# Layer 1 of a four-layer graph network: the new gate and the self terms worked out in the banks of their products

## The chip, the cores and the metric

The kernel runs on one core of a Trainium2 chip. The time is device time in microseconds (us), the median of several executions; lower is better. One execution was also taken by the hardware profiler. Engines: PE multiplies matrices (fp32 here), DVE and ACT work elementwise, POOL issues the indirect DMAs, SP issues plain ones. PE writes to PSUM, which has eight banks of 128 x 512 fp32 numbers; POOL and the DMAs work on SBUF and DRAM.

## The reference

Four layers over one graph of 6250 nodes and 106250 edges, each with a layer norm and a relu ahead of it and a residual. The change lies in layer 1 and in the products for layer 2 that the same loop makes:

```python
# layer 1, h = relu(layernorm(x)); both directions of every edge are in the list
input_in  = segment_mean((h @ W_in.T + b_in)[src], dst)
input_out = segment_mean((h @ W_out.T + b_out)[dst], src)
gi = concat(input_in, input_out) @ W_ih.T + b_ih
gh = h @ W_hh.T + b_hh
reset = sigmoid(i_r + h_r);  inp = sigmoid(i_i + h_i)
new = tanh(i_n + reset * h_n)
x = x + (1 - inp) * h + inp * new

# layer 2, h = relu(layernorm(x)); 8 relations r
hW = einsum('nd,rde->rne', h, weight)
x = x + h @ sl_w.T + sl_b + segment_sum(hW[edge_type, src], dst) / max(deg, 1)
```

All tensors are fp32 with 256 features.

## The kernel before, in words

The nodes are sorted by their number of edges into 49 blocks of 128, and each block has a fixed number of slots per node (CAPS, 39 down to 9, 822 in all; a node's edge to itself is left out of the slots). After a stage that builds the lists, stages f0 to f3 are the layers 0 to 3. In each stage POOL issues one indirect DMA for each block and slot (L1110): 128 rows of a table in DRAM, one to each partition.

Stage f1 is layer 1. The two weight matrices of each direction have been folded into one, wc. The blocks are taken from the one with fewest slots to the one with most. Five steps, written as generators, stand a block apart, so that in round k block k is summed, block k-1 multiplied, and so on:

- sums: eight gathers fill a buffer v (seven buffers); DVE adds the rows in a tree (L1383, L1386, L1390), and compares neighbour lists for a check of the graph ("mirror": L1176, and L1181 to L1188 at the block's end).
- products: the total is scaled (L1399, L1400) and a bias row made (L1402); PE transposes h and the total; then PE makes the gate products pg (h and total, 512 columns), ph and pi (256 columns each: h's and the total's part of the new gate), each in a PSUM tile of kind "g".
- gates: DVE adds biases (L1425, L1427, L1428), ACT takes the sigmoid, DVE works out the new gate (L1434, L1435, after ACT's tanh L1438, L1439), adds it to the residual xt (L1433, L1440), and takes the statistics of the next norm; ACT makes h2 (L1452).
- messages: PE transposes h2 and multiplies it by the weights of the eight relations, two at a time (L1462), and ACT moves each pair out of PSUM into res (L1463), which SP stores to DRAM for layer 2's gathers. Then PE makes the own product (L1468), and DVE adds its bias and the product to xt (L1470, L1471).
- selves: a node's edges to itself: for each of eight relations DVE adds res times a factor per node to xt (L1476). SP stores xt (L1480).

The order on PE, DVE and ACT is the order in which the program is written (manual_schedule), with waits put in by the framework; L1492 lists, by letters s, p, g, m and o, how the steps of a round are dealt out, and L1494 what finishes them. POOL and SP run ahead as buffers allow. The eight PSUM banks of f1 are two of kind "t" (transposes), three of kind "g" and three of kind "m" (messages and the own product). At the end of f1 "judge" (L1216) sums up the check; layer 2's first gather comes after it.

Of the kernel before, what the change touches and what calls it, by code (L numbers as in the profile page):

```python
# [8 lines left out]
F32 = mybir.dt.float32  # L9
# [3 lines left out]
ALU = mybir.AluOpType  # L13
# [4 lines left out]
P = 128  # L18
# [8 lines left out]
D = 256  # L27
H = 8
DH = 32
R = 8  # L30
# [1189 lines left out]
def sparse(ctx: ExitStack, tc: tile.TileContext, S, qv_d, rows_d, wc_d, bc_d, b_ih, w_hh,  # L1220
           b_hh, w_rel, w_sl, b_sl, w_gat, att_src, att_dst, b_gat, gamma, beta, out):

    nc = tc.nc
    K = Fast(ctx, tc)
# [125 lines left out]


    rel_idx = K.c([P, NB, J], I32, "rel_idx")
    with K.stage("f1", t=2, g=3, m=3), tc.tile_pool(name="f1w", bufs=1) as wp, tc.tile_pool(name="f1", bufs=2) as pool:
        wc = K.weights(wp, wc_d, "wc")
        wh = K.weights(wp, w_hh, "w_hh")
        wr = K.weights(wp, w_rel, "w_rel")
        ws = K.weights(wp, w_sl, "w_sl")
        bc = K.row(wp, bc_d.rearrange("a n -> (a n)"), 3 * D, "bc")
        bi = K.row(wp, b_ih, 3 * D, "b_ih")
        bh = K.row(wp, b_hh, 3 * D, "b_hh")  # L1360
        nc.vector.tensor_add(bi[:, : 2 * D], bi[:, : 2 * D], bh[:, : 2 * D])
        bs = K.row(wp, b_sl, D, "b_sl")
        rel_rows = rel_d[: NP * R, :].rearrange("(n r) d -> n (r d)", r=R)
        mirror = Mirror(K, S, wp)
        state = {}

        nothing = lambda *a: iter(())
        order = list(range(NB - 1, -1, -1))

        def sums(i):  # L1370

            h = pool.tile([P, D], F32, name="hb", tag="hb", bufs=4)
            nc.sync.dma_start(h, K.block(h1_d, i)[:, :D])
            xt = pool.tile([P, D], F32, name="xb", tag="xb", bufs=7)
            nc.sync.dma_start(xt, K.block(x1_d, i))
            total = pool.tile([P, D], F32, name="total", tag="total", bufs=3)
            state[i] = dict(h=h, xt=xt, ins=total)
            for c, n in S.chunks(i, 8):
                v = S.fill(pool, "v", 7, h1_d, i, c, n, 8, HW, S.idx)
                m = n  # L1380
                while m > 2:
                    k = m // 2
                    nc.vector.tensor_add(v[:, :k, :D], v[:, :k, :D], v[:, m - k: m, :D])  # L1383
                    m -= k
                if m == 2:
                    nc.vector.tensor_add(total if c == 0 else v[:, 0, :D], v[:, 0, :D], v[:, 1, :D])  # L1386
                elif c == 0:
                    nc.vector.tensor_copy(total, v[:, 0, :D])
                if c:
                    nc.vector.tensor_add(total, total, v[:, 0, :D])  # L1390
                mirror.found(i, c, n, v[:, :n, D:])
                yield
            mirror.block(i)

        def products(i):

            h, ins = state[i]["h"], state[i]["ins"]

            nc.vector.scalar_tensor_tensor(ins, h, S.own[:, i: i + 1], ins, op0=ALU.mult, op1=ALU.add)  # L1399
            nc.vector.tensor_scalar(ins, ins, S.rcnt[:, i: i + 1], None, op0=ALU.mult)  # L1400
            ba = pool.tile([P, 3 * D], F32, name="ba", tag="ba")
            nc.vector.scalar_tensor_tensor(ba, bc, S.has[:, i: i + 1], bi, op0=ALU.mult, op1=ALU.add)  # L1402
            yield
            pt = K.ps([P, 4, P], "t")
            for k in range(4):
                nc.tensor.transpose(pt[:, k, :], (h, ins)[k // 2][:, k % 2 * P: (k % 2 + 1) * P], K.ident)
            both = pool.tile([P, 4, P], F32, name="hit", tag="hit")
            nc.scalar.activation(both, pt, AF.Copy)
            ht, it = both[:, :2, :], both[:, 2:, :]
            yield  # L1410
            pg = K.ps([P, 2 * D], "g")
            K.product(pg, ht, wh[:, :, : 2 * D], stop=False)
            K.product(pg, it, wc[:, :, : 2 * D], start=False)
            ph = K.ps([P, D], "g")
            K.product(ph, ht, wh[:, :, 2 * D:])
            pi = K.ps([P, D], "g")
            K.product(pi, it, wc[:, :, 2 * D:])
            state[i].update(ba=ba, pg=pg, ph=ph, pi=pi)

        def gates(i):  # L1420

            x = state[i]
            h, xt, ba = x["h"], x["xt"], x["ba"]
            g = pool.tile([P, 2 * D], F32, name="g", tag="g")
            nc.vector.tensor_add(g, x["pg"], ba[:, : 2 * D])  # L1425
            new = pool.tile([P, D], F32, name="new", tag="new")
            nc.vector.tensor_add(new, x["ph"], bh[:, 2 * D:])  # L1427
            nc.vector.tensor_add(ba[:, 2 * D:], ba[:, 2 * D:], x["pi"])  # L1428
            yield
            nc.scalar.activation(g, g, AF.Sigmoid)  # L1430
            yield

            nc.vector.tensor_add(xt, xt, h)  # L1433
            nc.vector.tensor_mul(new, new, g[:, :D])  # L1434
            nc.vector.tensor_add(new, new, ba[:, 2 * D:])  # L1435
            nc.scalar.activation(new, new, AF.Tanh)
            yield
            nc.vector.tensor_sub(new, new, h)  # L1438
            nc.vector.tensor_mul(new, new, g[:, D:])  # L1439
            nc.vector.tensor_add(xt, xt, new)  # L1440
            st = pool.tile([P, 6], F32, name="st", tag="st")
            nc.vector.bn_stats(st, xt)
            mv = pool.tile([P, 2], F32, name="mv", tag="mv")
            nc.vector.bn_aggr(mv, st)
            rs = pool.tile([P, 1], F32, name="rs", tag="rs")
            nc.scalar.activation(rs, mv[:, 1:2], AF.Sqrt, bias=K.eps)
            yield
            nc.vector.reciprocal(rs, rs)
            nm = pool.tile([P, 1], F32, name="nm", tag="nm")
            nc.vector.tensor_scalar(nm, mv[:, 0:1], rs, -1.0, op0=ALU.mult, op1=ALU.mult)  # L1450
            h2 = pool.tile([P, D], F32, name="h2", tag="h2")
            nc.scalar.activation(h2, xt, AF.Relu, bias=nm, scale=rs)  # L1452
            x["h2"] = h2

        def messages(i):
            x = state[i]
            x["h2t"] = K.transposed(pool, x["h2"], "h2t")
            yield
            res = x["res"] = pool.tile([P, R, D], F32, name="res", tag="res")
            for r in range(0, R, 2):  # L1460
                pm = K.ps([P, 2 * D], "m")
                K.product(pm, x["h2t"], wr[:, :, r * D: (r + 2) * D])  # L1462
                nc.scalar.activation(res[:, r: r + 2, :].rearrange("p a b -> p (a b)"), pm, AF.Copy)  # L1463
                if r == 2:
                    yield
            nc.sync.dma_start(K.block(rel_rows, i), res.rearrange("p r d -> p (r d)"))
            pm = K.ps([P, D], "m")
            K.product(pm, x["h2t"], ws)  # L1468
            yield
            nc.vector.tensor_add(x["xt"], x["xt"], bs)  # L1470
            nc.vector.tensor_add(x["xt"], x["xt"], pm)  # L1471

        def selves(i):
            xt, res = state[i]["xt"], state[i]["res"]
            for r in range(R):
                nc.vector.scalar_tensor_tensor(xt, res[:, r, :], S.ownr[:, i, r: r + 1], xt, op0=ALU.mult,  # L1476
                                               op1=ALU.add)
                if r == 3:
                    yield
            nc.sync.dma_start(K.block(x2_d, i), xt)  # L1480
            del state[i]

        with tc.manual_schedule(engines={nc.tensor.engine, nc.vector.engine, nc.scalar.engine}):
            for k in range(NB + 4):
                s, p, g, m, o = (f(order[k - d]) if 0 <= k - d < NB else nothing()
                                 for d, f in enumerate((sums, products, gates, messages, selves)))
                if k == 4:  # L1490
                    nc.vector.scalar_tensor_tensor(rel_idx, S.idx, float(R), S.types, op0=ALU.mult, op1=ALU.add)
                for step in (g, p, m, p, g, s, m, g, o, s, m, p, g, s, o, g):  # L1492
                    next(step, None)
                for step in (s, m, p, g, o):  # L1494
                    for _ in step:
                        pass
            mirror.judge(S.bad, S.todo)
# [3 lines left out]
    with K.stage("f2", t=2, m=4, a=2), tc.tile_pool(name="f2w", bufs=1) as wp, tc.tile_pool(name="f2", bufs=2) as pool:  # L1501
        w = K.weights(wp, w_gat, "w_gat")
# [4 lines left out]
        for i in range(NB):  # L1507
# [6 lines left out]
            xt = pool.tile([P, D], F32, name="xb", tag="xb")  # L1514
# [7 lines left out]
            pm = K.ps([P, D], "m")  # L1522
# [11 lines left out]
    with K.stage("f3", m=2, a=2, w=2), tc.tile_pool(name="f3w", bufs=1) as wp, tc.tile_pool(name="f3", bufs=2) as pool:  # L1534
# [3 lines left out]
        o = wp.tile([P, NB, D], F32, name="o", tag="o")  # L1538
# [6 lines left out]
        for i in range(NB):  # L1545
            n = P if i < NB - 1 else NLAST
# [246 lines left out]
```

## Time and profile before

| what | value |
|---|---|
| median of 3 runs | 5667.33 us (5661.75 to 5673.34) |
| the profiled execution's own time | 4971.87 us |
| its span, first to last instruction | 4970.0 us |
| busy share of the span | POOL 69%, PE 61%, DVE 55%, ACT 17% |
| gathers of layer 1, first start to last end | 1578.9 to 2686.6 us |
| first gather of layer 2 | 2744.9 us |

The profiled execution is 14% shorter than the runs that were timed; the profile has no record of those, so its durations are of the profiled one alone. A line of a group reads: line, engine, operation, what it writes <- what it reads (partitions x elements), count | busy us, mean ns of one | idle time ahead of it and who ended it. A line of the timeline reads: start us, length us, engine, line, operation.

### The profile page before, as it was taken

What the parts mean: (1) busy time and instruction counts of PE and PEld (TensorE: products, weight loads), DVE (VectorE), ACT (ScalarE), POOL (GpSimd) and SP (SyncE); (2) the same over time, 40 slices, a digit from 0 to 9 for tenths busy, and PEclk for the clock granted to TensorE, in tenths of its full rate; (3) what the DMA queues carried; (4) which work ended last, traced back from release to release, by engine and by line L of the source; (5) the groups of instructions that cost most, each with busy time, mean ns of one, the idle gap of its engine ahead of it and who ended that gap; (6) DMA issues with size and microseconds to landing.
All of it is one profiled execution on the core that took longest, in us unless ns stands there. A gap on an engine that the chain in (4) does not pass through costs nothing. (4 is left out here: it accounts for less than half of the span.)

```text
span 4970.0 us, 34096 instructions
## 1 busy us (share of the span) xinstructions
PE 3019.2 (61%) x9191; PEld 1861.4 (37%) x9192; DVE 2730.3 (55%) x5064; ACT 865.4 (17%) x1808; POOL 3444.3 (69%) x3538
## 2 busy tenths in 40 slices
PE   5863544444444888776555778788873555555560
PEld 4532433333333444433322334344441444444450
DVE  6853888888886889877766111111121434343443
ACT  1231111222222444333222000000110000000000
POOL 1254777777774777777774677777776777777766
PEclk9976777777766898887777676766776777777785
DMA  3446777888885566555553344444445444444431
GB/s 106 120 157 202 224 231 233 233 237 236 239 238 167 182 191 190 181 170 170 169 159 112 119 121 119 122 123 125 127 128 164 110 112 115 114 115 115 116 101 52
DMA packets 328336, 776.03 MB, mean 156 GB/s; under 512 B 87439, under 2 KB 172299, under 8 KB 321607
## 3 DMA queue, kind: packets, MB, share of 16 engines
q0 software_dynamic: 196864, 595.62, 42.3%
q1 hardware_dynamic: 110904, 162.80, 9.4%
q10 hardware_dynamic: 20367, 15.35, 1.0%
q8 instruction: 76, 1.25, 0.1%
q14 instruction: 125, 1.02, 0.1%
HBM read 638.29 MB, written 135.19 MB: 156 GB/s over the span
## 5 line engine op out<-in xcount | busy, mean ns | idle before, releaser
L1110 POOL DMA_INDIRECT v<-h,rec_in x822 | 856.7, 1042 | 250.7 <-issue 232.1
L1110 POOL DMA_INDIRECT v<-rel,rel_idx x822 | 782.8, 952 | 308.5 <-issue 238.9
L1110 POOL DMA_INDIRECT v<-xa,rec_in x822 | 779.1, 948 | 268.7 <-issue 227.9
L1110 POOL DMA_INDIRECT qv<-qv,rec_in x822 | 779.2, 948 | 255.4 <-issue 200.8
L1513 PE MATMUL ps_a<-v,ident 128*128 128x256 f32 x1644 | 767.7, 574 | 206.4 <-DMA v<-rel,rel_idx 189.9
L1513 PEld LDWEIGHTS ps_a<-v,ident 128*128 128x128 f32 x1644 | 351.2, 258 | 587.5 <-DMA v<-rel,rel_idx 532.8
L1571 PE MATMUL ps_a<-v,ident 128*128 128x256 f32 x1644 | 449.5, 435 | 33.3 <-DVE v L1569 33.3
L1297 PE MATMUL ps_a<-qv,ident 128*128 128x256 f32 x1644 | 454.0, 444 | 8.7 <-DVE qv L1295 8.6
L1292 PE MATMUL ps_a<-row,ident 128*128 128x256 f32 x98 | 59.7, 713 | 628.1 <-DVE row L1291 628.1
L538 PE MATMUL ps_m<-w_rel,h2t 128*128 128x512 f32 x784 | 426.5, 706 | 1.1 <-ACT h2t L531 1.1
L1297 PEld LDWEIGHTS ps_a<-qv,ident 128*128 128x128 f32 x1644 | 370.0, 229 | 108.3 <-DVE qv L1295 43.9
L1571 PEld LDWEIGHTS ps_a<-v,ident 128*128 128x128 f32 x1644 | 362.9, 223 | 118.6 <-DVE v L1569 56.4
L1553 DVE TENSOR_TENSOR s<-v,asd 128x64 f32<-128x64 f32 (+7 forms) x124 | 26.4, 213 | 604.1 <-DMA v<-xa,rec_in 595.9
L1259 DVE TENSOR_TENSOR tmp<-qv,ps_k 128x1280 f32<-128x1280 f32 (+4 forms) x183 | 247.0, 1350 | 178.1 <-ACT ps_k L1253 85.1
L1383 DVE TENSOR_TENSOR v<-v 128x512 f32<-128x512 f32 (+2 forms) x211 | 187.6, 889 | 184.1 <-DMA v<-h,rec_in 157.6
L1292 PEld LDWEIGHTS ps_a<-row,ident 128*128 128x128 f32 x98 | 24.5, 310 | 647.9 <-DVE row L1291 574.0
L1527 DVE TENSOR_TENSOR tmp<-att,xa 128x512 f32<-128x512 f32 x49 | 34.2, 697 | 416.7 <-ACT xa L1525 416.7
L538 PEld LDWEIGHTS ps_m<-w_rel,h2t 128*128 128x128 f32 x784 | 178.9, 235 | 217.5 <-issue 205.7
L1566 PE MATMUL ps_a<-xh,ident 128*128 128x256 f32 x98 | 49.2, 598 | 342.5 <-DVE xh L1564 260.5
L1260 DVE TENSOR_REDUCE s<-tmp 128x40 f32<-128x1280 f32 (+4 forms) x183 | 247.1, 1351 | 6.3
L1516 DVE SCALAR_TENSOR_TENSOR xb<-ps_a,rcnt_in,xb 128x256 f32<-128x256 f32 x49 | 23.7, 483 | 409.8 <-PE ps_a L1513 409.8
L1295 DVE TENSOR_TENSOR qv<-qv,ps_w 128x1280 f32<-128x1280 f32 (+4 forms) x183 | 235.0, 1344 | 0.0
(285 smaller groups left out, 4555.8 us busy)
## 6 DMA issues: line engine op xcount, KB each, us to landing
rel<-res SPq DMA_DIRECT2D x49, 1024.0 KB
rows<-mrow SPq DMA_DIRECT2D x49, 512.0 KB
fx<-xb SPq DMA_DIRECT2D x147, 128.0 KB
qv<-qv,rec_in POOLq DMA_INDIRECT x822, 3.8
v<-h,rec_in POOLq DMA_INDIRECT x822, 3.1
v<-rel,rel_idx POOLq DMA_INDIRECT x822, 2.7
v<-xa,rec_in POOLq DMA_INDIRECT x822, 2.8
qv<-mrow ACTq DMA_DIRECT2D x49, 256.0 KB
```

The lines of the kernel that those rows point to most:

```text
L538: self.nc.tensor.matmul(out, xt[:, k, :], w[:, k, :], start=start and k == 0, stop=stop and k == n - 1)
L1110: self.nc.gpsimd.indirect_dma_start(out=out, out_offset=None, in_=table, in_offset=bass.IndirectOffsetOnAxis(ap=idx, axis=0))
L1259: nc.vector.tensor_mul(tmp[:, :n, :], qv[:, :n, :D], pk[:, None, :].to_broadcast([P, n, D]))
L1260: nc.vector.tensor_reduce(s[:, c: c + n, :], tmp[:, :n, :].rearrange("p j (h d) -> p j h d", h=H), axis=AX.X, op=ALU.add)
L1292: nc.tensor.matmul(pm, K.ident, row[:, 2, :], start=True, stop=False)
L1295: nc.vector.tensor_mul(v, v, w[:, c: c + n, :, None].to_broadcast([P, n, H, DH]))
L1297: nc.tensor.matmul(pm, K.ident, qv[:, j, D: 2 * D], start=False, stop=c + j == nd - 1)
L1383: nc.vector.tensor_add(v[:, :k, :D], v[:, :k, :D], v[:, m - k: m, :D])
L1513: nc.tensor.matmul(pa, K.ident, v[:, j, :], start=c + j == 0, stop=c + j == nd - 1)
L1527: nc.vector.tensor_mul(tmp, att, xa[:, None, :D].to_broadcast([P, 2, D]))
L1566: nc.tensor.matmul(pm, K.ident, xh, start=True, stop=False)
L1571: nc.tensor.matmul(pm, K.ident, v[:, j, :D], start=False, stop=c + j == nd - 1)
```

## The change

```diff
-    with K.stage("f1", t=2, g=3, m=3), ...
+    with K.stage("f1", t=2, g=3, m=2, w=1), ...
...
-            ph = K.ps([P, D], "g")
+            both = K.ps([P, 2 * D], "g")
+            ph, pi = both[:, :D], both[:, D:]
             K.product(ph, ht, wh[:, :, 2 * D:])
-            pi = K.ps([P, D], "g")
             K.product(pi, it, wc[:, :, 2 * D:])
...
-            new = pool.tile([P, D], F32, name="new", tag="new")
-            nc.vector.tensor_add(new, x["ph"], bh[:, 2 * D:])
+            new = x["ph"]
+            nc.vector.tensor_add(new, new, bh[:, 2 * D:])
...
             nc.sync.dma_start(K.block(rel_rows, i), res.rearrange("p r d -> p (r d)"))
-            pm = K.ps([P, D], "m")
+            yield
+            pm = x["pm"] = K.ps([P, D], "w")
             K.product(pm, x["h2t"], ws)
             yield
-            nc.vector.tensor_add(x["xt"], x["xt"], bs)
-            nc.vector.tensor_add(x["xt"], x["xt"], pm)
+            nc.vector.tensor_add(pm, pm, bs)
+            nc.vector.tensor_add(pm, pm, x["xt"])

         def selves(i):
-            xt, res = state[i]["xt"], state[i]["res"]
+            xt, pm, res = (state[i][n] for n in ("xt", "pm", "res"))
             for r in range(R):
-                nc.vector.scalar_tensor_tensor(xt, res[:, r, :], S.ownr[:, i, r: r + 1], xt, op0=ALU.mult,
-                                               op1=ALU.add)
+                nc.vector.scalar_tensor_tensor(pm if r < R - 1 else xt, res[:, r, :], S.ownr[:, i, r: r + 1], pm,
+                                               op0=ALU.mult, op1=ALU.add)
...
-                for step in (g, p, m, p, g, s, m, g, o, s, m, p, g, s, o, g):
+                for step in (g, p, m, p, g, s, m, g, o, s, m, p, g, o, s, m, g):
                     next(step, None)
-                for step in (s, m, p, g, o):
+                for step in (s, o, m, p, g):
```

The new gate has no SBUF tile of its own any more: it is worked out, tanh included, in the half bank where its product with h lies, and the two 256-column products share a bank. The own product has a bank of its own ("w"), in which bias, xt and seven of the self terms are added; the eighth writes the sum to xt in SBUF. The messages' banks are two. In a round, the second half of the self terms comes ahead of the third step of the sums, and the own product, a step of its own now, after that and so behind the products of the next block.

More of the change, by code (lines that the diff above doesn't have):

```diff
@@ L1352, in sparse @@
     rel_idx = K.c([P, NB, J], I32, "rel_idx")
-    with K.stage("f1", t=2, g=3, m=3), tc.tile_pool(name="f1w", bufs=1) as wp, tc.tile_pool(name="f1", bufs=2) as pool:
+    with K.stage("f1", t=2, g=3, m=2, w=1), tc.tile_pool(name="f1w", bufs=1) as wp, tc.tile_pool(name="f1", bufs=2) as pool:
         wc = K.weights(wp, wc_d, "wc")
```

## The prediction, made before the changed kernel was run

> **What bounds the kernel now.** The chain that ended last is no help here (it names only the last scatter), so I read the page's busy shares, then its costliest groups, then the stretches of layer 1, the waits in it, and its timeline.
>
> ```profile
> PE 3019.2 (61%) x9191; PEld 1861.4 (37%) x9192; DVE 2730.3 (55%) x5064; ACT 865.4 (17%) x1808; POOL 3444.3 (69%) x3538
> ...
> L1110 POOL DMA_INDIRECT v<-h,rec_in x822 | 856.7, 1042 | 250.7 <-issue 232.1
> L1110 POOL DMA_INDIRECT v<-rel,rel_idx x822 | 782.8, 952 | 308.5 <-issue 238.9
> L1110 POOL DMA_INDIRECT v<-xa,rec_in x822 | 779.1, 948 | 268.7 <-issue 227.9
> L1110 POOL DMA_INDIRECT qv<-qv,rec_in x822 | 779.2, 948 | 255.4 <-issue 200.8
> ```
>
> Each of the four layers issues the same 822 gathers on POOL. In layer 1 (v<-h) one takes 1042 ns on average, elsewhere about 950.
>
> ```profile
> core 0: us, PE busy (x) PEld busy (x) DVE busy (x) ACT busy (x) POOL busy (x), PEclk, DMA share, GB/s
> 1578.90:2060.00 481.10, 375.51 (x1006) 193.44 (x1006) 409.86 (x911) 186.70 (x309) 371.61 (x378) 0.87 0.63 196
> 2060.00:2686.60 626.60, 382.42 (x970) 197.01 (x970) 458.80 (x964) 181.53 (x300) 485.80 (x463) 0.76 0.55 165
> 2686.60:2744.90 58.30, 33.78 (x84) 16.36 (x84) 39.62 (x89) 17.32 (x27) 0.00 (x1) 0.79 0.17 66
> ```
>
> The stretches are layer 1's short blocks, its long blocks, and the drain between its last gather and layer 2's first. DVE is busiest (85%) in the first, yet POOL never waits for it:
>
> ```profile
> POOL v L1110 <- issue: 232.1, 761, 0.5
> ...
> DVE v L1383 <- DMA v<-h,rec_in: 157.6, 44, 6.1
> ...
> POOL v L1110 <- DVE todo L1216: 58.3, 1, 58.3
> ...
> DVE same L1186 <- ACT own_slots L1183: 26.2, 22, 1.5
> ```
>
> POOL's gaps are issue gaps of 0.3 us; its one real wait is the 58.3 us drain. Layer 1 lasts 822 gathers x (0.945 + 0.305) = 1027 us, plus what stretches gathers, plus the drain. The first gather starts at 1578.9 and the last ends at 2686.6: 1107.7 us, so the stretching is 80 us. What stretches them is in the timeline:
>
> ```profile
> 2143.35 0.42 DVE L1439 TENSOR_TENSOR new<-new,g 128x256 f32<-128x256 f32 x1
> ...
> 2143.41 1.18 POOL L1110 DMA_INDIRECT v<-h,rec_in  x1 [0.30 <-issue]
> ...
> 2150.09 0.94 POOL L1110 DMA_INDIRECT v<-h,rec_in  x1 [0.30 <-issue]
> 2150.15 0.68 DVE L1425 TENSOR_TENSOR g<-ps_g,ba 128x512 f32<-128x512 f32 x1
> ...
> 2152.33 1.00 DVE L1402 SCALAR_TENSOR_TENSOR ba<-bc,has_in,b_ih 128x768 f32<-128x768 f32 x1
> ...
> 2152.60 1.55 POOL L1110 DMA_INDIRECT v<-h,rec_in  x1 [0.30 <-issue]
> ```
>
> A gather that reaches a point about 0.126 us after its start while DVE is inside an operation with two SBUF inputs stops until that operation ends. L1439 ends at 2143.77: 2143.77 - 2143.41 - 0.126 = 0.23, and the gather is 1.18 - 0.945 = 0.23 too long. L1402: 2153.33 - 2152.60 - 0.126 = 0.60; measured 0.60. L1425 has one input in PSUM; its gather is not stretched. Over the whole timeline, 304 of the 822 gathers run more than 20 ns over 945, and this rule gives each one's excess within 30 ns. Operations with a PSUM input (L1425, L1427, L1428, L1471) cover that point 63 times and stretch none.
>
> **What the skill says.** The Trainium skill, "SBUF — State Buffer", section "Who interferes with whom": "A DVE instruction with two SBUF inputs contends with a GpSimd instruction that reads SBUF"; the first to come holds the shared ports for its whole length, and one with at most one SBUF input, outside the two-port modes, does not contend. The trace agrees, number for number (above). "VectorE: DVE Perf Modes", "Rules for kernel authors", has elementwise work on a PSUM operand at one element a cycle; the trace agrees that this costs fp32 nothing:
>
> ```profile
> L1476 DVE SCALAR_TENSOR_TENSOR xb<-res,ownr,xb 128x256 f32<-128x256 f32 x392 | 191.2, 488 | 10.9
> ...
> L1516 DVE SCALAR_TENSOR_TENSOR xb<-ps_a,rcnt_in,xb 128x256 f32<-128x256 f32 x49 | 23.7, 483 | 409.8 <-PE ps_a L1513 409.8
> ```
>
> L1516 is the after-form of a self term, bar the output. In layer 2 it covers the gathers' point 18 times and stretches none.
>
> **The change, part by part.**
>
> *Inputs to PSUM.* Each block turns 14 DVE operations from two SBUF inputs into one of SBUF and one of PSUM: L1434, L1435, L1438, L1439, L1440, L1470 and the eight of L1476. Their count stays. Giving every stretched gather to the operation that covers its point, they hold: L1476 12.0 us (75 gathers), L1439 6.8 (29), L1435 2.3 (20), L1440 0.5, L1438 0.3, L1470 0.3; together 22.2 us. Others keep 58: L1383 31.6, L1402 14.5, L1176 3.1, the rest under 2.2 each. POOL bounds the stage, so a stretch removed is time removed: **-22.2**. A second estimate: if phases were even, an operation of length L would catch L²/(2 x 1.25) of stretch. Over the rows that is 58 us for the changed ones (392 x 0.095 + 294 x 0.071) and 125 for those that stay (81 L1383 of 1.22 us: 48; 100 of 0.69: 19; 49 L1402: 20; 259 adds of 0.42: 18; small ones 20). Measured is 80 of 183, a share of 0.44; 125 x 0.44 = 55 stays, so -25. I take the direct count, since a gather that arrives earlier may just wait longer for the same end of L1402 or L1383.
>
> *In-place in PSUM.* Reading and writing one bank in one DVE instruction is not in the trace. Writing alone is: L1288 into PSUM took 299 ns at 128 elements, L1277 into SBUF 293. Lower bound -10 ns each; upper +267 ns (a second pass over 256 elements), for 14 writes 3.7 us a block. I take +6 ns: 0.1 us a block, hidden, as DVE has room. A chunk's buffer is free 37 us or more before POOL writes it again (the least: 1738.6 to 1775.6, the end of the seventh earlier L1176 against the first gather). At the upper bound the 22 short blocks would cost 82 us, less 26 us of waits (next part), less 37 of room: 19 us reach POOL, and the gain is nearly gone. Tanh from PSUM to PSUM: ACT's 256-element copies took 384 ns out of PSUM and 369 into it, against 408: no cost.
>
> *The moved steps.* The second half of the self terms goes ahead of the third step of the sums. In the 22 short blocks that step is the mirror's, which waits on ACT (26.2 us over 22 times); 2.04 us of self terms now fill this. DVE shortens, POOL doesn't care: 0. On SP, L1480's store is issued a little earlier, in the same order against L1466 and the loads: 0.
>
> *The own product* moves behind the next block's products on PE, and waits for the last self term to free its one bank. Queued behind it are the transposes of h2, which wait for L1450 and L1452 anyway, later on DVE and ACT than that self term. L1470 now waits for it: PE ends the own product about where the gate products ended before, 0.3 to 2.7 us ahead of L1470 in short blocks, over 3.6 in long ones. Cost 0, or at most some 0.8 us of DVE in seven blocks, inside the 37 us. In the drain nothing covers it: L1470 (0.42), done early before, now follows the last product, and in the round with the last gate products L1425 comes later, pushing L1434 by about 0.3. **+0.8**, between 0 and 3.
>
> *Banks.* Two for the messages: the third pair needs the first one's eviction. In the tightest case seen that ends at 1720.0 and the third pair begins at 1720.2; PE has 207.7 us of waits on h2. 0. New and input products share one bank, so three "g" banks hold one and a half blocks; the bank wanted was freed a round earlier. 0.
>
> Sum: -22.2 + 0.8 = **-21.4**. The profiled execution took 4971.87 us (span 4970.0), so its successor should take 4950. The runs' median, 5667.33, is 695 us above it and the profile doesn't show why; I carry the difference over unscaled (scaled by 5667/4972 it would be -24): 5667.3 - 21.4 = 5646.
>
> **Rivals.** About 0.2% (11 us) is what a measurement of this kernel can tell from no change.
> - *The rest takes it back* (no change, 5663): gathers come earlier at L1402 and L1383 and are let go at the same ends. At a share of 0.6, 75 us remain: -5 + 0.8. For it: L1402 covers 41 points in 49 blocks. Against: layer 2's two such operations (13 us if even) show 5.3, a share of 0.40.
> - *More than counted* (5629): reordered DVE work leaves a share of 0.33, 41 us: -39 + 0.8. For it: short blocks follow a period set by DVE (18.6 to 19.5 us), which the filled ACT wait shortens.
> - *Slower* (5688): the same re-phasing the other way. Now the 0.69 us adds catch 0.6 us of an even 19, because they follow the 1.22 us ones at once; if gathers fall evenly on L1383 and L1402, a share of 0.8 leaves 100 us: +20 + 0.8. It decides from 0.73 on (91 us); break-even is 0.63.
>
> **How the numbers follow.** Forecast 0.58 (own range 5634 to 5656), taken back 0.18, more 0.12, slower 0.12. Faster 0.58 + 0.12 = 0.70; same 0.18; slower 0.12. The range 5625 to 5670 takes in the first three cases (and the in-place bound) and leaves out the slower one and some tails.
>
> **What would show it.** Right: the v<-h gathers' mean falls from 1042 to about 1015 ns, no L1434 to L1440, L1470 or L1476 stretches one, their own lengths stay within 10 ns, and the drain is 58 to 61 us. Wrong: that mean unchanged with L1402 and L1383 stretching more; in-place operations of 0.6 us and more, with POOL waiting for L1176; or PE's own product ended late before L1470.

## The result, and the profile after

The changed kernel took 5734.58 us (median of 4 runs, 5725.62 to 5744.7), the kernel before 5670.34 us (4 runs, 5661.75 to 5677.82) in the same rounds: a ratio of 1.011, with a 95% interval of 1.0086 to 1.0134. It is 64 us slower; the forecast was 21 us faster, with a range that ended at 5670.

One thing has to be known to read any number below: the same program takes one of two quite different times, and all the runs of a set, which share a chip, take the same one. In the six sets of runs below the kernel before had medians of 4972.2, 5605.6, 4972.3, 4972.3, 5659.1 and 4970.0 us, on the chips numbered 13, 6, 12, 1, 9 and 1. I call the first kind of chip short and the second long. That the chip itself decides it is likely but not shown: only chip 1 was met twice, short both times. By its time, the profile of before that the prediction was made from is of the short kind; the timed runs of the result, and the profile after (5739.23 us, span 5737.4), are of the long kind.

The page of the changed kernel, the same lines as were shown of before: busy shares, then the four layers' gathers (out <- in, count | busy us, mean ns of one | idle us ahead of them, and what ended most of it).

```profile
PE 2816.1 (49%) x9191; PEld 1880.0 (33%) x9192; DVE 2737.6 (48%) x5064; ACT 862.9 (15%) x1808; POOL 3396.5 (59%) x3538
...
L1110 POOL DMA_INDIRECT v<-h,rec_in x822 | 802.3, 976 | 559.0 <-DVE hits L1176 289.1
L1110 POOL DMA_INDIRECT v<-rel,rel_idx x822 | 785.8, 956 | 485.3 <-issue 232.6
L1110 POOL DMA_INDIRECT v<-xa,rec_in x822 | 780.4, 949 | 423.5 <-issue 229.9
L1110 POOL DMA_INDIRECT qv<-qv,rec_in x822 | 780.7, 950 | 417.6 <-issue 369.8
```

Two things are to be seen. In layer 1 (v<-h) a gather takes 976 ns instead of 1042, so most of the stretching that the change was priced on is gone. But POOL's idle time there is 559 us instead of 251, and in layers whose code did not change it is 155 to 177 us more as well (417.6 against 255.4 for qv). No engine is busy for more than 59% of the span. The waits of layer 1 (in total, times, longest, us):

```profile
PE ps_t L1406 <- DVE total L1400: 383.7, 37, 30.6
ACT h2t L531 <- remote: 338.0, 32, 29.6
POOL v L1110 <- DVE hits L1176: 289.1, 38, 15.0
DVE ps_w L1472 <- remote: 243.3, 29, 17.1
...
POOL v L1110 <- DVE todo L1216: 77.0, 1, 77.0
```

The third line is new against the profile before: POOL stops for the buffers v, which DVE gives back with L1176. The fourth names the longest of DVE's own waits: it stands at L1472, the first addition to the own product. "Remote" means that the releasing signal came at a moment at which the profile has no instruction ending. One such place in the timeline:

```profile
1943.42 1.03 PE L538 MATMUL ps_w<-w_sl,h2t 128*128 128x256 f32 x4
...
1944.28 0.38 PE L529 MATMUL ps_t<-ident,h 128*128 128x128 f32 x2
...
1944.50 0.38 PE L1406 MATMUL ps_t<-ident,hb 128*128 128x128 f32 x2
...
1948.06 0.95 POOL L1110 DMA_INDIRECT v<-h,rec_in  x1 [0.30 <-issue]
1950.81 0.43 DVE L1472 TENSOR_TENSOR ps_w<-ps_w,b_sl 128x256 f32<-128x256 f32 x1 [7.70 <-issue]
...
1951.59 0.38 ACT L531 ACTIVATE h2t<-ps_t 128x256 f32<-128x256 f32 x1 [7.85 <-remote]
...
1953.52 0.35 DVE L1400 TENSOR_SCALAR total<-total,rcnt_in 128x256 f32<-128x256 f32 x1
...
1953.93 0.69 PE L1406 MATMUL ps_t<-ident,total 128*128 128x128 f32 x2 [9.05 <-DVE total L1400]
```

The own product is recorded as ended at 1944.45 and the transposes of h2 at 1944.66, yet DVE starts on the one at 1950.81, 6.4 us later, and ACT on the other at 1951.59, 6.9 us later (for the first the profile names no releaser, for the second a remote one). The ends of matrix products in a profile are modelled, so by themselves these lines cannot tell a product that was finished late from one whose signal came late; the count further down comes back to this. Meanwhile PE has nothing to do: its next instruction waits for the total (L1400), which stands behind L1472 in DVE's queue. DVE waits for PE's last result and PE for DVE, until the signal comes.

The nearest counterpart is the kernel before on a long chip (the run b_fourth below, one execution of 5645.36 us, on chip 9). Its gathers and its waits in layer 1:

```profile
L1110 POOL DMA_INDIRECT v<-h,rec_in x822 | 844.9, 1028 | 442.5 <-issue 239.0
...
L1110 POOL DMA_INDIRECT qv<-qv,rec_in x822 | 780.5, 950 | 411.1 <-issue 372.3
```

```profile
PE ps_t L1406 <- DVE total L1400: 239.9, 28, 32.1
...
ACT h2t L531 <- remote: 213.0, 15, 32.3
POOL v L1110 <- DVE hits L1176: 196.1, 25, 18.2
...
POOL v L1110 <- DVE todo L1216: 93.8, 1, 93.8
...
DVE g L1425 <- remote: 82.9, 10, 14.8
...
DVE ba L1428 <- remote: 52.8, 12, 10.1
...
DVE new L1427 <- remote: 34.0, 8, 6.3
```

So before stops POOL there too. From layer 1's first gather to its last it took 1290.1 us, the changed kernel 1364.1 in its profile. The 74.0 us between them: the gathers' own time 802.3 - 844.9 = -42.6; pauses of POOL over 0.4 us 325.9 - 203.8 = +122.1; and 18 fewer plain gaps of 0.305, -5.5. The change did what it set out to do to the gathers, and nearly three times as much came back as stops. These are single executions of two runs, not made side by side; the ratio above is the measurement, the split only shows its kind.

### The profile page after: what moved, and what is told of

The parts are those of the page before. It is cut to its first block, busy times and chain, and to the rows that moved or that the text cites. A ratio compares the mean times of both kernels' runs of the same rounds, so it can differ in the third digit from the quotient of the medians.

```text
span 5737.4 us, 34048 instructions
## 1 busy us (share of the span) xinstructions
PE 2816.1 (49%) x9191; PEld 1880.0 (33%) x9192; DVE 2737.6 (48%) x5064; ACT 862.9 (15%) x1808; POOL 3396.5 (59%) x3538
## 5 line engine op out<-in xcount | busy, mean ns | idle before, releaser
L1110 POOL DMA_INDIRECT v<-h,rec_in x822 | 802.3, 976 | 559.0 <-DVE hits L1176 289.1
L1110 POOL DMA_INDIRECT qv<-qv,rec_in x822 | 780.7, 950 | 417.6 <-issue 369.8
L1297 PE MATMUL ps_a<-qv,ident 128*128 128x256 f32 x1644 | 510.1, 467 | 224.3 <-issue 200.8
L1573 PE MATMUL ps_a<-v,ident 128*128 128x256 f32 x1644 | 472.8, 441 | 132.4 <-issue 114.1
L538 PE MATMUL ps_m<-w_rel,h2t 128*128 128x512 f32 x784 | 454.7, 742 | 109.2 <-ACT res L1464 68.6
L1297 PEld LDWEIGHTS ps_a<-qv,ident 128*128 128x128 f32 x1644 | 388.8, 240 | 354.9 <-issue 261.6
L1515 PE MATMUL ps_a<-v,ident 128*128 128x256 f32 x1644 | 455.0, 431 | 64.7 <-issue 50.3
L538 PEld LDWEIGHTS ps_m<-w_rel,h2t 128*128 128x128 f32 x784 | 185.0, 246 | 346.6 <-issue 258.7
L1406 PE MATMUL ps_t<-ident,total 128*128 128x128 f32 x98 | 31.8, 424 | 440.9 <-DVE total L1400 383.7
L1571 DVE TENSOR_TENSOR v<-v,ps_w 128x2048 f32<-128x2048 f32 (+7 forms) x124 | 232.9, 1914 | 0.0
L538 PE MATMUL ps_m<-w_gat,ht 128*128 128x256 f32 x196 | 81.7, 560 | 305.1 <-ACT ht L531 175.2
L529 PE MATMUL ps_t<-ident,h 128*128 128x128 f32 x196 | 48.1, 333 | 344.4 <-ACT h L521 235.0
```

What stands on the lines that cost most here:

```text
L529: nc.tensor.transpose(pt[:, k, :], x[:, k * P: (k + 1) * P], self.ident)
L538: self.nc.tensor.matmul(out, xt[:, k, :], w[:, k, :], start=start and k == 0, stop=stop and k == n - 1)
L1110: self.nc.gpsimd.indirect_dma_start(out=out, out_offset=None, in_=table, in_offset=bass.IndirectOffsetOnAxis(ap=idx, axis=0))
L1297: nc.tensor.matmul(pm, K.ident, qv[:, j, D: 2 * D], start=False, stop=c + j == nd - 1)
L1515: nc.tensor.matmul(pa, K.ident, v[:, j, :], start=c + j == 0, stop=c + j == nd - 1)
L1571: nc.vector.tensor_mul(vv, vv, w[:, c: c + m, :, None].to_broadcast([P, m, H, DH]))
```

## The experiments

The theory, called the order theory below: on a long chip signals of PE come late, and the late own product makes DVE and PE wait for each other. Its rivals: two message banks are too few (bank theory); the sums held in the banks cost something (in-place, gate or self theory); or the change is slower on any chip. The expectations call the two kinds of chip conditions, and the rule of the stretched gathers the ports theory. Which kind of chip a set would meet could not be chosen, so some kernels appear in several sets. Every set has its own runs of the kernel before.

**First set, a short chip: before as it is, and the parts alone.** Before is unchanged in b_again. The run called gate has the new gate in its bank, which its two products share, and nothing else:

```diff
-            ph = K.ps([P, D], "g")
+            both = K.ps([P, 2 * D], "g")
+            ph, pi = both[:, :D], both[:, D:]
             K.product(ph, ht, wh[:, :, 2 * D:])
-            pi = K.ps([P, D], "g")
...
-            new = pool.tile([P, D], F32, name="new", tag="new")
-            nc.vector.tensor_add(new, x["ph"], bh[:, 2 * D:])
+            new = x["ph"]
+            nc.vector.tensor_add(new, new, bh[:, 2 * D:])
```

The run called order has only the banks and the order:

```diff
-    with K.stage("f1", t=2, g=3, m=3), ...
+    with K.stage("f1", t=2, g=3, m=2, w=1), ...
...
-            pm = K.ps([P, D], "m")
+            yield
+            pm = x["pm"] = K.ps([P, D], "w")
...
-                for step in (g, p, m, p, g, s, m, g, o, s, m, p, g, s, o, g):
+                for step in (g, p, m, p, g, s, m, g, o, s, m, p, g, o, s, m, g):
...
-                for step in (s, m, p, g, o):
+                for step in (s, o, m, p, g):
```

The run called self is order with the self terms summed in the own product's bank (new lines alone):

```diff
+            nc.vector.tensor_add(pm, pm, bs)
+            nc.vector.tensor_add(pm, pm, x["xt"])
...
+                nc.vector.scalar_tensor_tensor(pm if r < R - 1 else xt, res[:, r, :], S.ownr[:, i, r: r + 1], pm,
```

Expected of b_again:

> The kernel before, unchanged, profiled again beside the others. Theory P (the profile that the prediction was read from shows an execution that differs from the timed ones): its span comes out near 5670 us and not near 4970, its matmuls start tens of us after their gathers as in the changed kernel's profile, and layer 1's gathers take about 1290 us from first to last (1364 in the changed kernel, less the 64 us by which that is slower). Rival (the changed kernel alone has these waits): a span near 4970 and gathers of layer 1 in about 1108 us.

Of gate:

> Only the new gate is worked out in PSUM (new and input products in one bank); self terms, message banks and order as before. Ports theory (a gather waits for a vector operation with two SBUF inputs, and that is what counts): 5 to 10 us faster than before, about 5662. Order theory (the loss comes from the own product behind the next block's products, on which the vector engine then waits): no change, 5670 within 11 us. If the in-place work in PSUM itself were slow: slower by 10 us or more.

Of order:

> Only the order and the banks of the change: the own product has a bank of its own, the messages have two, the own product comes behind the next block's products, the second half of the self terms ahead of the third step of the sums; all vector operations keep their SBUF operands. Ports theory: no change, 5670 within 11 us. Order theory: slower by 60 to 90 us, about 5735 to 5760.

Of self:

> Order and banks as in the changed kernel and the self terms in PSUM; the new gate in SBUF with three banks for its products as before. Ports theory: 10 to 15 us faster than before, about 5657. Order theory: as slow as the changed kernel, 5730 within 15 us.

Measured: before 4972.16 us (29 runs, 4965.77 to 4976.21), b_again 4971.63. gate 4957.24, a ratio of 0.9969 (0.9957 to 0.998); order 4976.96, 1.0011 (1.0002 to 1.0019); self 4961.24, 0.9981 (0.9973 to 0.9989). It follows that the profile of before was no odd execution: this program takes 4972 us on such a chip, time after time. The expectations' absolute times, made for a chip on which before takes 5670, do not apply here. The parts follow the stretching in direction and roughly in size. The gathers' stretch in one profile of each, taken as time over 945 ns, was 76.7 us in b_again, 65.7 in gate, 68.6 in self, and 83.6 in order: -11.0, -8.1 and +6.9, where the times changed by -14.9, -10.9 and +4.8. The run order has no new PSUM input and only moves work: its self terms hold 15.5 us instead of 11.8 and its L1383 33.4 instead of 29.5.

**Second set, a long chip: the changed kernel again, and with an early own product.** early_own is the changed kernel with this:

```diff
-            yield
             pm = x["pm"] = K.ps([P, D], "w")
...
-                for step in (g, p, m, p, g, s, m, g, o, s, m, p, g, o, s, m, g):
+                for step in (g, p, m, p, g, s, m, g, o, o, s, m, p, g, s, g):
```

> The changed kernel, unchanged. Condition theory (the same program takes 4972 us in one condition of the chip and 5670 in the other; the change saves stretched gathers in the one, and in the other loses to a mutual wait of VectorE and TensorE around the own product): where before takes about 4972, the single parts run so far (-15 and -11) add up to about 4946 (-20 to -30 us); where before takes about 5670, again about 5735. Rival (the change is slower everywhere, by something that only the parts together have): slower than before by 40 us or more in either condition.

> The changed kernel with the own product issued right behind the h2 transposes again, ahead of the next block's message products, and its bias and old-feature adds ahead of both halves of the self terms; the new gate and the self terms still in their banks, two message banks. Order theory: where before takes about 5670, VectorE finds the own product done and this kernel takes 5640 to 5670, 65 to 95 us less than the changed kernel. Bank theory (two message banks) or the in-place sums: it stays near 5735 there. Where before takes about 4972, all theories: 4943 to 4955, within 5 us of the changed kernel.

Measured: before 5605.58 us (9 runs), after_again 5652.65 (5647.81 to 5658.55), a ratio of 1.0086 (1.0061 to 1.0112); early_own 5639.74 (5626.78 to 5650.14), 1.0064 (1.0045 to 1.0084). The loss is there again, 47 us. But by the order theory the early own product was to give the loss back (65 to 95 us had been expected), and early_own is only 13 us below after_again, with 4 and 6 runs whose ranges overlap, and still 34 above before. As the whole cause the late own product falls, and its share is not clear of noise. What DVE waited for longest in layer 1 of after_again, and then the waits of early_own:

```profile
DVE ps_w L1472 <- remote: 161.0, 26, 15.1
```

```profile
PE ps_t L1406 <- DVE total L1400: 359.5, 35, 36.8
ACT h2t L531 <- remote: 285.7, 17, 40.7
...
POOL v L1110 <- DVE hits L1176: 212.5, 33, 14.3
...
DVE g L1425 <- remote: 146.8, 13, 18.7
...
DVE ps_g L1428 <- remote: 55.8, 6, 21.0
```

The long wait at the own product is gone (32.7 us in 7 times at L1471, which was L1472 in after_again), and DVE now waits nearly as long for the gate products, at L1425, where after_again had 14.5 us in one wait. The lateness is not tied to the own product; it moved to another result of PE. In these two profiles layer 1 with its drain lasts 1365.5 us in early_own against 1408.0, a difference of 42.5, while the whole executions are 16.6 us apart: the other stages, the same in both, differ by 26 the other way. Single profiles of long chips vary that much.

**Third set, a short chip: message banks alone.** banks is before with this:

```diff
-    with K.stage("f1", t=2, g=3, m=3), ...
+    with K.stage("f1", t=2, g=3, m=2, w=1), ...
...
-            pm = K.ps([P, D], "m")
+            pm = K.ps([P, D], "w")
```

> Only the split of the banks: two for the messages, one for the own product, which keeps its place ahead of the next block's products; all else as before. Where before takes 5600 or more: bank theory (TensorE waits for ScalarE's evictions): slower by 25 to 45 us; order theory: within 10 us of before. Where before takes 4972: within 5 us of it by all theories.

Before, order and gate were repeated in the same set:

> The kernel before, unchanged: one look, to have its trace beside the others' in the condition in which it takes 5600 to 5670 us. Condition theory: its layer 1 is stretched there too (first gather of layer 1 to first gather of the attention's layer about 1300 to 1350 us, 1166 in the profile shown before), with waits for buffers that the profile before does not have, but fewer than in the changed kernel. Rival: layer 1 takes the 1166 us of the profile before, and only other stages are longer.

> Only the order of the own product and the split of the banks (two for the messages, one for the own product); the new gate and the self terms as before. Where before takes 5600 or more: order or bank theory: slower by 30 to 50 us, nearly the whole loss of the changed kernel (47 on this chip); in-place theory (the sums in the banks lose it): within 15 us of before. Where before takes 4972: +5, as before.

> Only the new gate worked out in the bank of its products. Where before takes 5600 or more: order and bank theories: between 0 and 25 us faster than before, as the port's share of it is 15 us where before takes 4972; in-place theory: slower by 10 us or more, since the bank is held from its product until the new state is written. Where before takes 4972: -15 again.

Measured, with before at 4972.34: banks 4971.28 (1.0, 0.9992 to 1.0009), b_slow 4971.53, order_slow 4977.43 (1.0011, 1.0005 to 1.0018), gate_slow 4959.94 (0.9974, 0.9965 to 0.9982). Two message banks cost nothing on a short chip, so the 5 us of order belong to the order of the work. On a long chip the banks alone were not run. What the traces show there is that PE's waits for ACT to empty a message bank are 68.6 us with two banks (the profile after), and 48.1 and 63.1 us with three (b_fourth, and gate_fourth of the fifth set): no large cost of the second bank is to be seen, and none is excluded.

**Fourth set, a short chip: the whole change where the prediction's profile was taken.**

> The changed kernel, unchanged. Where before takes 4972: the parts add up to about -26 (-20 to -30), 4942 to 4952; a loss there would say that the parts hinder each other. Where before takes 5600 or more: slower by 40 to 65 us again.

> Only the order of the own product and the split of the banks. Where before takes 5600 or more: order theory: slower than before by 30 us or more. Gate or self theory (holding the banks in place loses it): within 15 us of before. The early own product took back 13 of the 47 us there, so I now take 10 to 20 us of loss as likeliest. Where before takes 4972: +5 again.

> Only the new gate worked out in the bank of its products. Where before takes 5600 or more: order theory: 0 to 25 us faster than before; gate theory: slower by 15 us or more. Where before takes 4972: -13 to -15 again.

> The kernel before, unchanged, one look for its trace. Where it takes 5600 or more: layer 1 about 1240 to 1300 us from its first gather to its last (1108 in the profile shown before; 1325 and 1364 in the changed kernel's), with GpSimd stopped for value buffers in it.

Measured, with before at 4972.33: after_third 4957.75 (11 runs, 4951.22 to 4964.85), 0.9971 (0.9962 to 0.998), 14.6 us faster; order_third 4977.8 (1.0011), gate_third 4959.52 (0.9975, 0.9968 to 0.9982), b_third 4974.18. The parts do not add up to the whole: gate alone gains 12.8, order with the self terms gained 11, both together 14.6, less than the 20 to 30 that had been expected. The page's line and layer 1's waits of after_third:

```profile
L1110 POOL DMA_INDIRECT v<-h,rec_in x822 | 836.7, 1018 | 250.8 <-issue 232.1
```

```profile
POOL v L1110 <- issue: 232.1, 761, 0.5
...
DVE v L1383 <- DMA v<-h,rec_in: 155.7, 45, 8.5
...
POOL v L1110 <- DVE todo L1216: 57.5, 1, 57.5
...
DVE ps_w L1472 <- PE ps_w L538: 15.7, 11, 3.7
```

POOL never stops but in the drain, and DVE waits for gathered data: here the gathers bound the layer, as the prediction had it. (1018 ns for a gather and 57.5 us for the drain are close to its signs of being right, about 1015 ns and 58 to 61 us.) The timeline shows where a gather is stretched and where not, with the work in the banks:

```profile
2180.84 2.05 DVE L1478 SCALAR_TENSOR_TENSOR ps_w<-res,ownr,ps_w 128x256 f32<-128x256 f32 x4
2180.92 0.95 POOL L1110 DMA_INDIRECT v<-h,rec_in  x1 [0.31 <-issue]
...
2186.67 1.95 DVE L1383 TENSOR_TENSOR v<-v 128x1024 f32<-128x1024 f32 x2 [3.77 <-DMA v<-h,rec_in]
2187.18 1.53 POOL L1110 DMA_INDIRECT v<-h,rec_in  x1 [0.30 <-issue]
...
2190.21 0.43 DVE L1440 TENSOR_TENSOR ps_g<-ps_g,g 128x256 f32<-128x256 f32 x1
2190.27 0.95 POOL L1110 DMA_INDIRECT v<-h,rec_in  x1 [0.30 <-issue]
```

Under four self terms and under the new gate's last product a gather takes its 0.95 us; under the wide addition of two SBUF operands it takes 1.53. Counted as in the prediction, by the point 0.126 us after a gather's start, the changed operations held 21.4 us in b_third, where they cover that point 222 times and stretch 134 of these gathers by over 20 ns. In after_third they hold 0.7 us and cover it 199 times, and none of these gathers is longer by more than 13 ns. The whole stretch fell from 76.4 to 59.9 us, by 16.5 and not by 20.7: 4.2 came back at other operations, above all at L1383 (29.6 to 36.5), while L1402 held less.

**Fifth set, a long chip: the gate alone, and before's trace.**

> Only the new gate worked out in the bank of its products. Where before takes 5600 or more: if the gate's banks lose the time there, slower by 15 us or more; if the order, the message banks or the self terms do, 0 to 25 us faster than before. Where before takes 4972: -13 to -15 again.

> The kernel before, unchanged, one look for its trace. Where it takes 5600 or more: layer 1 about 1240 to 1300 us from its first gather to its last, with GpSimd stopped for value buffers by VectorE's hits (none of it in the profile shown before, 247 us in the changed kernel's where that takes 5650). Where it takes 4972: as before.

Measured: before 5659.08 us (14 runs, 5649.3 to 5671.53); gate_fourth 5682.96 (11 runs, 5666.19 to 5707.8), a ratio of 1.004 (1.0024 to 1.0056); b_fourth 5645.36. The same edit that gains 12 to 15 us in three sets on short chips loses 24 here (14 to 32 by the interval), on the one long chip that it met. Nothing of the own product is moved in it. Its gathers:

```profile
L1110 POOL DMA_INDIRECT v<-h,rec_in x822 | 816.7, 994 | 484.7 <-issue 236.2
```

Against b_fourth they take 28.2 us less, and POOL's pauses over 0.4 us grew from 203.8 to 251.1 us. The time that was saved on POOL became waiting, and more. That does not yet place the loss: the two profiled executions are 29 us apart, and only 4 of these lie in layer 1 with its drain (1387.7 us against 1383.9 from its first gather to the next layer's), the rest in stages that the edit does not touch; executions of one kernel range over 22 and 42 us on this chip. Nor is the bank, held for longer, seen to stop PE: before the gate products PE idles 10.8 us in gate_fourth and 11.2 in b_fourth. One thing did change in layer 1. As both products share a bank, the first addition waits for the second product too: L1427 has 89.5 us of remote waits and L1428 none, where b_fourth has 34.0 and 52.8, much the same sum.

**Last set, a short chip.** self_early is the run self with the own product early, as in early_own.

> Only the order of the own product and the split of the banks. Where before takes 5600 or more: the changed kernel lost 47 there, the gate alone 24 and the early own product took 13 back, so if the parts add up the order costs 10 to 25 us; if it stays within 5 us, the loss of the changed kernel is the gate's and the self terms'. Where before takes 4972: +5 again.

> Only the self terms in the own product's bank, which is issued ahead of the next block's products as before; two banks for the messages; the new gate in SBUF as before. A version that may serve in both conditions. Where before takes 4972: 4955 to 4965 (the self terms' share of the stretched gathers, without the order's +5). Where before takes 5600 or more: within 12 us of before, if the gate's bank (+24) and the late own product (+13) are what the changed kernel loses by; slower by 15 us or more if the self terms in the bank or the two message banks lose it too.

Measured, with before at 4970.04: order_fifth 4975.99 (1.0012, 1.0005 to 1.0019), self_early 4962.24 (0.9982, 0.9974 to 0.999). On a short chip self_early gains 7.8 us and self gained 10.9, the same within their intervals: the place of the own product makes no difference that can be told to the self terms' gain. Neither kernel met a long chip, so their shares of the loss there stay open. The changed kernel and gate, which met both kinds of chip, gain on the short and lose on the long; whether self or self_early would do better on the long is not known.

**Late signals, counted.** The traces in hand allow a count for layer 1. I took each result of PE (messages, own product, gate products, both kinds of transposes) that ACT or DVE had stood waiting for over 1 us, and the time from the recorded end of its last matmul to the start of the one who waited; late means over 3 us. I split them by whether PE begins another matmul between 0.7 and 3 us after that end; these limits were chosen with the traces in view.

| run (chip) | PE goes on: late of all | PE stands: late of all |
|---|---|---|
| b_third (short), before | 0 of 141 | 0 of 3 |
| after_third (short), changed | 0 of 140 | 0 of 8 |
| b_fourth (long), before | 24 of 155 | 37 of 41 |
| gate_fourth (long), gate alone | 26 of 149 | 40 of 44 |
| early_own (long) | 29 of 170 | 25 of 28 |
| after_again (long), changed | 30 of 162 | 60 of 74 |
| the profile after (long), changed | 25 of 160 | 62 of 72 |

On the short chips no result comes more than 0.1 us after its end. On the long ones a result behind which PE has more work mostly comes at once (134 of 796 are late), and one after which PE stands is nearly always late (224 of 259), by up to 40 us. But the split is a tendency and not a rule. In the unchanged layer 2 of after_again:

```profile
3291.18 0.69 PE L529 MATMUL ps_t<-ident,h 128*128 128x128 f32 x2 [16.00 <-issue]
...
3291.66 1.91 PE L1515 MATMUL ps_a<-v,ident 128*128 128x256 f32 x4
...
3306.01 0.95 POOL L1110 DMA_INDIRECT v<-rel,rel_idx  x1 [0.30 <-issue]
3313.05 0.38 ACT L531 ACTIVATE ht<-ps_t 128x256 f32<-128x256 f32 x1 [21.93 <-remote]
```

The transposes are recorded as ended at 3291.87 and ACT takes them at 3313.05, though PE went on with four more products until 3293.57. From 3306.96, when the last gather's issue ends, until 3313.05 no engine does anything.

Nor does the count follow the loss. The changed order has 74 and 72 waits behind which PE stands, before has 41; but early_own has 28, fewer than before, and still loses 34 us to it, and gate_fourth has 44 and loses 24.

The traces also list the moments of the signals themselves, and these tell late products from late signals. In b_third PE's 3218 signals are never closer than 0.109 us to each other, as close as the ends of PE's products come. In b_fourth 2612 are listed, and 772 of them follow the one before within 0.06 us, although the recorded ends are nowhere closer than 0.108. In the example of 1943 to 1954 us above, three results end between 1944.45 and 1944.88, and the next signals of PE that are listed stand at 1951.51 and 1951.55 (the one on which DVE began at 1950.81 is not listed). Nor is a single product longer: the median of the message products (L538) is recorded as 592 ns in both runs, though the mean granted clock is lower on the long chip (0.715 against 0.747). So results of PE seem to be held back and announced together. One caution belongs to this: on the long chips the list has gaps (2615 signals of DVE in b_fourth, 4688 in b_third), so who released a wait is less certain there than on a short chip. The starts of the instructions, from which the table is made, do not depend on it.

## Why the prediction was wrong, by its own steps

- *The difference to the median "carried over unscaled", with "POOL bounds the stage, so a stretch removed is time removed".* This is the step that failed. The prediction saw that the timed runs were 695 us longer than the profiled one and that the profile did not show why, and then priced the change as if those 695 us lay outside everything it touched. b_fourth shows that they lie in every layer: from first gather to last, layers 0 to 3 take 1243.8, 1290.1, 1179.0 and 1169.3 us there, and 1086.3, 1103.7, 1033.0 and 1032.0 in b_third. In layer 1 POOL pauses for 203.8 us instead of 1.0 (pauses over 0.4 us), waiting for buffers that DVE gives back late, and DVE itself waits for results of PE. So POOL does not bound layer 1 in the timed runs, and a stretch removed is not time removed: the 28.2 us (gate_fourth) and 42.6 us (the profile after) that the gathers saved against b_fourth came back as pauses, and more. The room that was to cover every small cost is gone as well: a buffer v had been free 31.5 us or more before POOL wrote it again in b_third, but for less than 1 us in 29 of 117 cases in b_fourth, and in 48 of 117 in the profile after. (The 37 us that the prediction read as the least was a misreading: in its own trace the least is 31.4, from 1596.2 to 1627.6.)
- *Inputs to PSUM, -22.2.* Right as a mechanism on both kinds of chip: the changed operations hold 0.7 us (after_third) and 0.5 us (the profile after) of stretch where they held 21.4 and 23.3. As a time it held in part on the short chips, -14.6 (interval -18.9 to -9.9): "the rest takes it back" happened for 4.2 of the 20.7 us. The forecast for an execution like the profiled one, 4950, was 8 us too low. The rule of the stretch was read only one way: it gives the excess of gathers that are stretched, but not which are. In the profile before, the point lies at least 40 ns ahead of the end of a self term (L1476) 140 times, and only 74 of these gathers are stretched; those self terms began 89 ns or more before the gather, and the 66 others later than 94 ns before it.
- *The own product, "cost 0".* Right on short chips, where L1472 waits 15.7 us for it in all and no buffer is missed. On long chips L1472 waits 243.3 us in the profile after and 161.0 in after_again. Taking the move back gave 13 of 47 us, not clear of noise, as DVE then waited at L1425 instead. So the wait was mis-sized there, but how much of the loss is its doing stays open.
- *Banks, 0,* and *in-place work, +6 ns*: right on short chips. In after_third two of the new gate's operations (L1436, L1440) take 432 and 433 ns, where b_third has 425 and 426 (L1435, L1439), and the self terms 484 instead of 487. On a long chip the gate in its bank loses 24 us though none of its operations grew by more than 12 ns; why, no run shows.
- *Drain, +0.8*: 57.5 us in after_third against 58.8 in b_third; no cost.

Two of the signs that the prediction had named for being wrong came true in the profile after: POOL waits for L1176 (289.1 us), and the own product comes late to the addition that takes it. The slow in-place operations that it tied to the first did not.

What is shown: the change gains on short chips by the named mechanism and loses on long ones; the gate's edit alone loses on the one long chip that it met; and results of PE reach DVE and ACT late there, also in the unchanged kernel. What stays open: why signals come late on some chips; in which stage the gate's 24 us are lost; and how the whole loss divides between the gate, the order, the self terms and the message banks, since order, self, banks and self_early met short chips only and the gate's loss is from another chip than the 47 us. The link from the late signals to the loss is argued from traces, and no run removed the lateness alone.

## What to carry to other kernels

Hold the profiled execution's own time against the timed runs before pricing anything: if they are 14% apart, the profile may show another bound than the one that decides, and an execution from the timed kind has to be looked at, or the forecast has to carry both signs. Here, moving DVE's operands to PSUM freed the gathers that ran beside it, at some 7 ns for an addition or a product of 256 columns, and it saved time only where the gathers bound the stage. Where DVE's queue, which keeps its order, waits for the last thing that PE does, and PE's next work waits behind it on DVE, as at 1943 to 1954 us above, a late signal stops both. Whether more work on PE behind a result that is waited for would help was not tried by itself: the table speaks for it, the case in layer 2 against it.

## What the runs showed of the hardware that was not expected

- One program, two times: 4970 to 4972 us in four sets and 5606 to 5670 in three, each within 0.5% in itself, with a mean granted TensorE clock of 0.740 to 0.753 in the runs of before of the one kind and 0.714 to 0.721 in the other.
- On the long chips 224 of 259 results of PE after which PE stood, and 134 of 796 others, started their waiting reader 3 to 40 us after their recorded end; on the short ones none started more than 0.1 us after it. PE's signals come in bursts there: 772 of 2612 within 0.06 us of the one before (b_fourth), none of 3218 in b_third.
- An addition or a product in place in a PSUM bank took 432 ns for 256 columns, against 425 in SBUF; tanh from bank to bank took 376 ns against 409 (after_third, b_third).
